# Attention and selective scan on one core: the convolution folded into u's weights, side results used a step later, one product with B per unit

## The chip, the core and the metric

The kernel runs on one core of one Trainium2 chip. The metric is device time in microseconds (us) of one execution of the whole program, all 16 images included. Five engines matter: PE (TensorE: matmuls, with PEld for its weight loads), DVE (VectorE), ACT (ScalarE), POOL (GpSimd) and SP (SyncE), which issues the DMA transfers here. SBUF and PSUM are the core's two on-chip memories; matmuls write PSUM. "f32 128x512" is a tile of 128 partitions with 512 elements each.

## The reference, cut to what matters

The input x is (16, 256, 32, 32). Two layers follow each other, each on a group-normalised x and added to x:

```python
x = x + _L0_conv_ref(_gn(x), ...)   # attention and a feed-forward part
x = x + _L1_conv_ref(_gn(x), ...)   # a selective scan with a gate
```

With 32 x 32 positions there are L = 1024 tokens of 256 channels. Layer 0 adds a position embedding and has layer norm, four heads of attention, layer norm and two feed-forward products with gelu. Layer 1 is, cut to its core:

```python
xs = xs + pos
ctx = sigmoid(conv1d(xs, gate_w, width 3) + gate_b)
xz = xs @ in_proj_w.T
u, z = split(xz, 2)                       # 512 channels each
uc = causal depthwise conv(u, conv_w, width 4) + conv_b
u = silu(uc)
dt, Bm, Cm = split(u @ x_proj_w.T, [16, 80])
delta = softplus(dt @ dt_proj_w.T + dt_proj_b)
A = -exp(A_log)                           # 512 x 64
def step(h, inp):                         # over the 1024 tokens
    dA = exp(d_t[..., None] * A)
    h = dA * h + (d_t * u_t)[..., None] * B_t[:, None, :]
    y = einsum('bdn,bn->bd', h, C_t)
y = (ys + u * D) * silu(z)
return (y @ out_proj_w.T) * ctx
```

## The kernel before, in words

**The main loop.** The scan has 512 channels x 64 states x 1024 steps for every image. It is cut into units: for each of the 16 images (b), 2 halves of the tokens (t), 4 blocks of 128 channels (k), 4 quarters of a block (q) and 8 groups (i): 256 units per image, 4,096 in all. A unit scans four channels over 512 tokens: two instructions of 128 partitions (two channels x 64 states each) x 512. In iteration n the loop body issues, in this order: `load(n+6)`, `inputs(n+4)`, the two scans of unit n, `decay(n+2)`, then steps of the side work, then the steps of the output generators that are running.

- `load` fetches delta*u of the unit's channels, repeated over the 64 states, in one DMA of 512 KB into `dub` (L859, seven buffers), and at block edges B, C and the pieces of delta.
- `inputs` multiplies `dub` by B on POOL, in place, in two instructions of 128x512, one for each scan (L869).
- `decay` makes delta*A: two matmuls that pick rows out of `pieces` (L878) into two of four PSUM buffers, and two Exp on ACT in place (L881).
- `scan` runs the recurrence on DVE: h = a*h + dub (L891), into one of two h buffers.
- `outputs`, once per eight units, forms y = C*h: 128 small matmuls per half (L928) against the spread C (`cd`), a copy on ACT (L936), small matmuls that turn the result (L940), a copy to `yo` (L948) and four stores on SP (L954), a step apart.
- `spread_c` makes `cd` once per t: eight ACT instructions in unit 6 (L907). When t is 0 a memset of the whole `cd` on POOL goes first (L903). The PSUM tile `yb` is cleared on DVE per t (L918).

**The side work.** While image b is scanned, the main loop also prepares image b+1 and finishes image b-1. This is one chain of generators: `first_norm` (group norm), `gate_and_store(b-1)` (output product and gate), `attention_layer`, `scan_inputs`. Each `yield` in them carries a share of work; the loop advances the chain at an even rate, so that a step falls into about every unit, and all of it ends before the image's last units. Image 0 is prepared alone, before the first scan (the prologue); the last image's loop has only `gate_and_store` beside it.

All of PE, ACT, DVE and POOL keep the order in which the program issues (a dependency is added from each instruction to the next of its engine at the end of the program). So an instruction that waits holds up everything behind it on its engine. SP's order is set by the scheduler.

**Lines that the change and the prediction touch.** In `group_norm` the variance goes through Ln and Exp on ACT (L260 to L261) and is used by DVE (L264) one step later; `layer_norm` has means (`ln_m`, matmuls L272), differences (L279), variances (`ln_v`, L272), Ln and Exp (L298) and the products (L303); `gate_and_store` adds u*D and gates by z (L787, L791), makes the output product (`m_ps`, L816) and finishes it (L803, L805). In `scan_inputs`:

- z: per 128 channels and half, two matmuls (L607), Tanh on ACT (L612), and DVE's product (L596), issued at the next half's start. L584 adds the position before.
- u: per 128 channels and half two matmuls (L628), a copy with three zeros ahead of it (L633) and the last tap with its bias on ACT (L634); then three taps of 128x1024 on DVE (L642), Tanh on ACT (L679) and one product on DVE (L682).
- the gate's convolution: eight groups of 12 matmul instructions and a bias (L657, L661), beside the taps.
- dt, B and C: `x_ps` (L694, L698).
- softplus and the pieces of delta, per 128 channels: matmul (L713), ACT (L715, L722, L739), DVE (L726, L727, L743, L748, L752, L756) and stores on SP.

PSUM has eight banks: four for the decays (`aps`), one for `yb`, one `accp` for the attention's accumulation, two (`mm`) for all other side matmuls through `psum`. `wide` has ten buffers of 128 x 1030.

## Time and profile before

| what | value |
|---|---|
| median of four runs | 13,538.78 us (13,537.11 to 13,545.84) |
| the profiled execution, its own time | 13,537.89 us |
| its span (first to last instruction) | 13,536.1 us |
| granted TensorE clock, mean | 0.767 |
| busy PE, PEld | 10,665.2 us (79%), 5,378.5 us (40%) |
| busy DVE | 12,099.6 us (89%) |
| busy ACT | 7,914.7 us (58%) |
| busy POOL | 10,458.8 us (77%) |
| DMA | 2,821.36 MB, 208 GB/s over the span |

How to read what follows: a group line of the profile has the source line, the engine, the operation, output and inputs with their shapes, the number of executions; after the first bar the busy time in us and the mean of one in ns; after the second bar the engine's idle time just before these instructions, and what ended most of it. "<-POOL dub L869" means that the engine idled until POOL's instruction of line 869 had written `dub`. A window line has its bounds in us from the span's start, its length, then busy time and number of instructions for each engine, the granted PE clock (1.00 is full speed), the share of the DMA engines' time, and GB/s. A timeline line has the start in us, the duration of the run of equal instructions, the engine, line and operation, their number, and in brackets the idle time before.

By the scans' places in the trace, the first scan starts at 387.8 us and the last ends at 13,488.1 us. The loop over the first image takes 794.6 us, over each of the images 1 to 14 about 831 us, and over the last 672.9 us.

### The profile page before, as it was taken

To read this page: it belongs to the slowest core of one execution; us is meant where nothing else is said; L and a number is where in the kernel's file an instruction comes from. 1 tells how busy PE (TensorE), PEld (TensorE's weight loads), DVE (VectorE), ACT (ScalarE), POOL (GpSimd) and SP (SyncE) were. 2 spreads that over 40 slices of the span, in tenths; PEclk is the share of its full clock that TensorE was granted. 3 is DMA by queue.
4 is the path that set the end of the run, shared out by engine and by line. 5 is a ranking of instruction groups with operands and counts; after the bars stand their busy time and mean duration, and the time that the engine had idled before them with its cause. 6 is when DMAs were issued, how large, how long until landed. Compare 5 with 4: busy or idle time off the path is not lost. (4 is left out here: it accounts for less than half of the span.)

```text
span 13536.1 us, 437083 instructions
## 1 busy us (share of the span) xinstructions
PE 10665.2 (79%) x186800; PEld 5378.5 (40%) x186800; DVE 12099.6 (89%) x11683; ACT 7914.7 (58%) x13941; POOL 10458.8 (77%) x8214
## 2 busy tenths in 40 slices
PE   7787878878787787877878778787887878878767
PEld 3343344433444334443344434434444343433434
DVE  3899999899998989999898998999998998899998
ACT  3666665656656566555656556566565665656644
POOL 0687877778777787877878778787787878778888
PEclk8786877868787686876868778687786877868767
DMA  1566566565665656656666566655666566566666
GB/s 60 198 212 233 196 214 217 201 230 202 208 219 202 224 200 213 216 203 225 205 228 202 199 222 206 233 197 202 221 209 234 194 213 216 203 231 202 205 218 224
DMA packets 1001958, 2821.36 MB, mean 208 GB/s; under 512 B 175810, under 2 KB 319427, under 8 KB 1000004
## 3 DMA queue, kind: packets, MB, share of 16 engines
q1 hardware_dynamic: 1000004, 2793.39, 60.5%
q8 instruction: 1460, 23.92, 0.7%
q14 instruction: 494, 4.05, 0.1%
HBM read 2514.18 MB, written 261.62 MB: 205 GB/s over the span
## 5 line engine op out<-in xcount | busy, mean ns | idle before, releaser
L869 POOL TENSOR_TENSOR dub<-dub,bt 128x512 f32<-128x512 f32 x8192 | 10403.6, 1304 | 3024.7 <-DMA dub<-dus 2641.2
L881 ACT ACTIVATE a<-a,acol 128x512 f32<-128x512 f32 x8192 | 5063.3, 659 | 3822.1 <-PE a L878 3790.8
L891 DVE TENSOR_TENSOR_SCAN h<-a,last,dub 128x512 f32<-128x512 f32 x4096 | 4927.4, 1261 | 130.9 <-POOL dub L869 72.6
L891 DVE TENSOR_TENSOR_SCAN h<-a,dub 128x512 f32<-128x512 f32 x4096 | 4692.3, 1201 | 283.3 <-POOL dub L869 212.3
L878 PE MATMUL a<-pieces,pick 48*128 48x512 bf16 x8192 | 2966.6, 467 | 2344.4 <-DVE h L891 2258.4
L928 PEld LDWEIGHTS yb<-h,cd 128*32 128x32 f32 x131072 | 2560.3, 135 | 2036.6 <-issue 1671.8
L928 PE MATMUL yb<-h,cd 128*32 128x64 f32 x131072 | 2957.9, 258 | 147.3 <-DVE yb L918 107.4
L878 PEld LDWEIGHTS <-pick 48*128 48x128 bf16 x8192 | 521.0, 96 | 2513.3 <-issue 2307.7
L403 PE MATMUL s_ps<-k,q 32*64 32x512 f32 x4096 | 888.2, 716 | 58.1 <-DVE mx L384 56.8
L940 PEld LDWEIGHTS yb<-turn,y 128*16 128x16 f32 x32768 | 409.4, 119 | 1011.3 <-ACT y L936 481.4
L936 ACT COPY y<-yb 128x256 f32<-128x256 f32 x1024 | 383.3, 374 | 716.2 <-PE yb L928 711.3
L384 DVE TENSOR_REDUCE mx<-s_ps 128x1 f32<-128x512 f32 x1024 | 644.3, 671 | 22.9 <-PE s_ps L403 20.5
L940 PE MATMUL yb<-turn,y 128*16 128x32 f32 x32768 | 539.2, 212 | 108.0 <-ACT y L936 97.5
L471 PE MATMUL st_ps<-sp 33*128 33x512 f32 x2048 | 598.4, 629 | 17.2 <-ACT pt L479 15.4
L459 PE MATMUL av<-pt,vv 128*64 128x512 f32 x2048 | 582.1, 647 | 5.6 <-ACT sums L448 3.3
L479 ACT ACTIVATE pt<-st_ps 128x512 f32<-128x512 f32 x1024 | 556.7, 605 | 48.2 <-PE st_ps L471 46.8
L657 PE MATMUL g_ps<-w,xp 128*128 128x256 f32 x1536 | 442.8, 443 | 0.0
L403 PEld LDWEIGHTS s_ps<-k,q 32*64 32x64 f32 x4096 | 206.9, 148 | 580.3 <-DVE mx L384 541.5
L657 PEld LDWEIGHTS g_ps<-w,xp 128*128 128x128 f32 x1536 | 387.0, 328 | 96.1 <-issue 74.6
L642 DVE SCALAR_TENSOR_TENSOR u<-up,cwh,u 128x1024 f32<-128x1024 f32 x192 | 295.3, 1538 | 32.7 <-ACT u L634 32.5
L816 PE MATMUL m_ps<-w,xs 128*128 128x256 f32 x1024 | 311.5, 453 | 13.2 <-DVE xs L791 13.2
L816 PEld LDWEIGHTS m_ps<-w,xs 128*128 128x128 f32 x1024 | 259.4, 328 | 90.1 <-issue 60.1
(135 smaller groups left out, 7128.9 us busy)
## 6 DMA issues: line engine op xcount, KB each, us to landing
dub<-dus SPq DMA_DIRECT2D x4096, 512.0 KB
dps<-pc SPq DMA_DIRECT2D x384, 128.0 KB
pieces<-dps SPq DMA_DIRECT2D x1024, 48.0 KB
xs<-in_x_dram SPq DMA_DIRECT2D x64, 512.0 KB
xs<-kept SPq DMA_DIRECT2D x64, 512.0 KB
zs<-z SPq DMA_DIRECT2D x64, 512.0 KB
ud<-u SPq DMA_DIRECT2D x64, 512.0 KB
dus<-du SPq DMA_DIRECT2D x64, 512.0 KB
```

Of the source, the lines that this page charges most:

```text
L384: nc.vector.tensor_reduce(mx[:, g, c, hf : hf + 1], s, AX.X, ALU.max)
L403: nc.tensor.matmul(waiting[g][0][ts(e, 64)], q4[r, ts(c, 64)], k4[r, hs(hf)], start=True, stop=True,)
L459: nc.tensor.matmul(av[ts(e, 2 * DH)], vv[j // (NJ // 2)][:, j % (NJ // 2), 2 * pair + e, :], pts[e], start=(j == 0), stop=(j == NJ - 1),)
L471: nc.tensor.matmul(s, ka[r, ts(j, P)], qa[r, hs(hf)], start=True, stop=True)
L657: nc.tensor.matmul(ps[:, ts(q, C)], xp[k][:, ds(first + t, P, 4)], wg_s[:, k, t, :], start=(i == 0), stop=False,)
L816: nc.tensor.matmul(ps[:, ts(q, C)], us[d][:, ds(first, P, 4)], wo_s[:, d, :], start=(d == 0), stop=(d == ND - 1),)
L869: nc.gpsimd.tensor_tensor(v, v, blocks[b, t]["bt"], ALU.mult)
L878: nc.tensor.matmul(a, w, pieces[r], start=True, stop=True)
L881: nc.scalar.activation(a, a, AF.Exp, scale=acol[:, at : at + 1])
L891: nc.vector.tensor_tensor_scan(now["h", q % 2][:, 2 * i + e, :], decays[n][e], loaded[n][:, e, :], first, ALU.mult, ALU.add,)
L928: nc.tensor.matmul(yb[ts(g, 32), ts(s, 64)], cd[:, at // 16, ts(c, 32)], hbuf[:, :, at : at + 4], start=(c == 0), stop=(c == 3),)
L940: nc.tensor.matmul(out4[32 * s : 32 * s + 16, half, e], y2[:, 64 * s + e : 64 * s + 64 : 4], turn[:, e], start=True, stop=True,)
```

## The change: what it does

- **u.** The depthwise convolution is linear, so it is moved into the input product: the prologue multiplies `w_in`'s columns for u by each of the four taps, on POOL, and stores the 4 x 512 KB of products in DRAM (`wcv`). Per image they are fetched one block at a time into a `wide` buffer (an eleventh is added), and `project` runs eight matmuls per block and half, on four shifted views of xs, in two groups of four with a step between them. Tanh and Identity on ACT and one product of 128x512 on DVE (`finish_u`, a step later) complete u. The copies, the taps and the 128x1024 product are gone, and `weights` fetches only z's half of `w_in`.
- **The gate's** matmuls move from the taps' steps to softplus, in pieces of three or four.
- **Side results a step later.** A `yield` is added between Ln/Exp and their use in `group_norm` and `layer_norm`; the two means of `layer_norm` get a bank each; z's product, m_ps's end and parts of softplus move one step on; `psum3` hands out the two `mm` banks and `accp` in turn for these.
- **B.** `inputs` issues one POOL instruction per unit, 128 x 2 x 512, with B repeated by a stride of zero.
- **cd and yb** are allocated and cleared once, in the prologue; the spread of C is divided over units 5 and 6.
- **Stores of y** are issued two steps later.

```diff
+    cd = hst.tile([P, TB // 16, P], F32, name="cd", tag="cd")
+    nc.gpsimd.memset(cd, 0.0)
...
+        t = work("wcs").rearrange("p (k t e) -> p k t e", k=KC, t=CONV)
+        for k in range(KC):
+            nc.gpsimd.tensor_tensor(
+                t[:, k], row[:, ts(d % 2, CONV * P)].rearrange("p (t e) -> p t e", t=CONV),
+                wu[:, k, ts(d, P)].unsqueeze(1).to_broadcast([P, CONV, P]), ALU.mult,
+            )
+        nc.sync.dma_start(wcv[ts(d, P), :], t.rearrange("p k t e -> p (k t e)"))
...
+    three = cycle((mm, mm, accp))
...
         nc.scalar.activation(v, v, AF.Exp, scale=-0.5)
-        yield 1.5
+        yield 1.2
+        yield 1
...
-        m = mean_of([t[:, hs(0)] for t in src], "ln_m")
-        yield 1
-        q0 = centre(0, m)
-        m = mean_of([t[:, hs(1)] for t in src], "ln_m")
+        m0 = mean_of([t[:, hs(0)] for t in src], "ln_m")
+        yield 0.7
+        m1 = mean_of([t[:, hs(1)] for t in src], "ln_m")
+        yield 0.7
+        q0 = centre(0, m0)
         yield 1.2
-        q1 = centre(1, m)
         vs = [mean_of(q0, "ln_v")]
+        q1 = centre(1, m1)
...
-                finish_z()
-                ps = psum("z_ps")
+                finish_z(1)
+                ps = psum3("z_ps")
...
-            ps = psum("u_ps")
-            for k in range(KC):
+            w = wcs[d].rearrange("p (k t e) -> p k t e", k=KC, t=CONV)
+            ps = psum3("u_ps")
+            for i in range(KC * CONV):
+                k, t = divmod(i, CONV)
                 nc.tensor.matmul(
-                    ps, win_s[:, k, ts(d, P)], body[k][:, hs(hf)],
-                    start=(k == 0), stop=(k == KC - 1),
+                    ps, w[:, k, t], xp[k][:, ds(hf * HL + t, HL)],
+                    start=(i == 0), stop=(i == KC * CONV - 1),
                 )
-            last = d * CONV + CONV - 1
-            nc.scalar.copy(ups[d][:, ds(CONV - 1 + hf * HL, HL)], ps)
-            nc.scalar.activation(
-                us[d][:, hs(hf)], ps, AF.Identity,
-                bias=cbh[:, d : d + 1], scale=cwh[:, last : last + 1],
-            )
+                if i == CONV - 1:
+                    yield 1.3
+            t = hwork("u_t")
+            nc.scalar.activation(t, ps, AF.Tanh, bias=cbh[:, d : d + 1])
+            nc.scalar.activation(ps, ps, AF.Identity, bias=cbh[:, d : d + 1])
+            ready.append((d, hf, t, ps))
...
-            items = [more(d, *items[0]), begin(d, 1)]
-            yield 1
+            items[0] = more(d, *items[0])
+            yield 0.8
+            items.append(begin(d, 1))
+            rest(*items[0])
+            yield 1.3
             items[1] = more(d, *items[1])
-            rest(*items[0])
-            yield 1.4
+            yield 0.8
             rest(*items[1])
...
+            gate(d // 2, d % 2, 0, 0)
             yield 1.4
...
-                    if q == 0:
+                    if q == 1:
                         finish()
...
-        for e in range(2):
-            v = loaded[n][:, e, :]
-            nc.gpsimd.tensor_tensor(v, v, blocks[b, t]["bt"], ALU.mult)
+        v, bt = loaded[n], blocks[b, t]["bt"]
+        nc.gpsimd.tensor_tensor(v, v, bt.unsqueeze(1).to_broadcast([P, 2, TB]), ALU.mult)
...
-        yield
+        for _ in range(3):
+            yield
...
-        if (k, q, i) == (0, 0, 6):
-            spread_c(b, t)
+        if (k, q) == (0, 0) and i in (5, 6):
+            spread_c(b, t, ((0, 1), (2, 3))[i - 5])
```

## The prediction

> **What bounds the kernel now.** I read the busy table first: DVE 12,099.6 of 13,536.1 us (89%), PE 79%, POOL 77%, ACT 58%. No engine is full, so I read DVE's waits next, then the stages, then single places. The costliest groups of the page:
>
> ```profile
> L869 POOL TENSOR_TENSOR dub<-dub,bt 128x512 f32<-128x512 f32 x8192 | 10403.6, 1304 | 3024.7 <-DMA dub<-dus 2641.2
> L891 DVE TENSOR_TENSOR_SCAN h<-a,last,dub 128x512 f32<-128x512 f32 x4096 | 4927.4, 1261 | 130.9 <-POOL dub L869 72.6
> L642 DVE SCALAR_TENSOR_TENSOR u<-up,cwh,u 128x1024 f32<-128x1024 f32 x192 | 295.3, 1538 | 32.7 <-ACT u L634 32.5
> ```
>
> A unit (two scans) needs 2 x 1.304 = 2.61 us of POOL and about 2.4 us of DVE; the scans wait little for POOL. DVE loses more in the side work, by shape:
>
> ```profile
> L726 DVE SCALAR_TENSOR_TENSOR d_ps<-sp_s,d_ps 128x512 f32<-128x512 f32 x128 | 88.4, 691 | 147.9 <-ACT d_ps L722 147.6
> L596 DVE SCALAR_TENSOR_TENSOR z<-z_t,z_ps 128x512 f32<-128x512 f32 x128 | 87.0, 680 | 96.3 <-ACT z_t L612 94.7
> L303 DVE TENSOR_TENSOR xn<-xn,ln_v 128x512 f32<-128x512 f32 x128 | 81.3, 677 | 105.1 <-ACT ln_v L298 105.1
> L264 DVE TENSOR_TENSOR gn<-gn,gn_v_ps 128x1024 f32<-128x1024 f32 x32 | 38.6, 1209 | 95.3 <-ACT gn_v_ps L261 95.3
> L803 DVE SCALAR_TENSOR_TENSOR m_ps<-xs,m_ps 128x512 f32<-128x512 f32 x64 | 44.5, 695 | 90.8 <-PE m_ps L816 90.8
> ```
>
> The last numbers are DVE's idle time: a side operation is placed in the same step as what it consumes, and since DVE keeps program order, the next scans queue behind it. Stage by stage, for image 6 (attention values; the u stage; x; softplus):
>
> ```profile
> core 0: us, PE busy (x) PEld busy (x) DVE busy (x) ACT busy (x) POOL busy (x), PEclk, DMA share, GB/s
> 5628.92:5773.05 144.13, 129.85 (x2638) 62.55 (x2638) 127.59 (x115) 119.63 (x229) 135.15 (x110) 0.94 0.66 221
> 5927.45:5998.10 70.65, 60.87 (x953) 39.48 (x953) 69.31 (x61) 40.08 (x67) 64.11 (x44) 0.91 0.57 189
> 5998.10:6022.93 24.83, 24.83 (x383) 13.38 (x382) 18.36 (x17) 11.24 (x21) 18.48 (x16) 0.97 0.56 199
> 6022.93:6147.99 125.06, 88.38 (x1536) 43.34 (x1535) 115.18 (x121) 90.65 (x151) 86.19 (x71) 0.56 0.60 202
> ```
>
> The bound changes: POOL leads the attention values (135.2 of 144.1), DVE the u stage (69.3 of 70.7), PE all of x, and in softplus DVE idles 9.9 of 125.1. Single places, from timelines:
>
> ```profile
> 6007.37 3.18 PE L694 MATMUL x_ps<-u,w 128*16 128x512 f32 x7
> ...
> 12839.00 3.51 POOL L903 MEMSET cd<- 128x4096 f32 x1
> ...
> 12845.61 4.57 DVE L891 TENSOR_TENSOR_SCAN h<-a,dub 128x512 f32<-128x512 f32 x4 [9.85 <-POOL dub L869]
> ...
> 12902.64 14.41 DVE L787 SCALAR_TENSOR_TENSOR xs<-xs,vec 128x1024 f32<-128x1024 f32 x1
> ```
>
> An f32 matmul of 512 columns is two PE instructions, and those of x start .43 us apart at full clock. The cd memset stops POOL, and DVE after it for 9.85 us. The xs operation, whose fastest execution is 1.25 us, took 14.4 us while POOL ran products without a break: its two inputs both lie in SBUF.
>
> **The change part by part, per image.** Fifteen images carry side work; each idle sum above is divided by 16, since the prologue or the last image adds a sixteenth.
>
> *Side results a step later.* The group norm's Ln and Exp get a whole step before DVE's multiply. Before: 95.3/16 = 6.0 (first norm), 42.2/16 = 2.6 (second). The cd memset, once per image, goes too, and its spread is halved over two units. I take -5.5 and -2.3; bounds are 0 and the rows. m_ps finished a step later: 5.7, I take -5. The layer norms (L303 6.6, L279's wait for ln_m 4.0) with q/k products a step apart: I take -6 for the first and -4 for the second with the steps around it; bounds 0 and -12.1 together, with f_ps's 24.6/16 = 1.5. z: 94.7/16 = 5.9, I take -5. Softplus, L726: 147.6/16 = 9.2, I take -7. None goes whole: the consumer is still in order on DVE, and what is late next is the scan's own inputs (POOL's product, the decay's exp).
>
> *Convolution in u's weights.* Out go 12 taps (1.51 us here) and four 1.31 us products, 23.3 us of DVE; in come eight 128x512 products at .68 like L596, 5.4. DVE of the u and x stages falls from 87.7 to about 69.8 us of 95.5. But PE gets 8 x 8 matmuls for 8 x 2: 128 instructions at .43 = 55.0 us against 13.8. The gates leave for softplus: eight of 12 instructions, 3.15 us each where they run together, 25.2. PE: 60.9 + 24.8 - 13.8 - 25.2 + 55.0 = 101.7 us, against 95.5 of wall. So the bound moves to PE and the saved DVE time is worth nothing: +5 (bounds 0, if the PE's records overlap as the modelled ends allow, and +10). Behind a group of four such matmuls (3.4 us) stand the next unit's decay matmuls, and behind those exp and scan; only two units of lead cover it. In softplus the gates' PE time fits (88.4 + 25.2 = 113.6 of 125.1), but at its clock of .56 a gate step can hold a decay for 3 us: +4 (0 to +13). u's weights arrive by four 512 KB fetches on SP ahead of need, while w_in's fetch is halved; the mean DMA share there is .57, so nothing, or +1 if a dub load waits behind one.
>
> *One product with B per unit.* A 128x1024 product with B repeated has no row. Least: 2 x 1.25 (the fastest halves) less a fixed .2 (the trace's smallest memsets take about .1) = 2.3; most: above 2 x 1.304 = 2.61. The repeat itself seems free: L264 repeats an operand and takes 1.21 us where L791's fastest is 1.19. I take 2 x 1.25 less one start of .1 = 2.40, nearest to the fastest halves. In the attention values 52 units x (2.50 - 2.40) = 5.2, and one join with its load instead of two: -6; v_ps a step later -2; the cd spread in two parts -2: -10 (-12 to 0). ACT at 119.6 and DVE at 127.6 of 144.1 are next.
>
> *The longer lock.* Sixteen DVE operations per image that read two SBUF inputs (L787, L791, L584, L330, L515) wait on average about .3 us for the running product (L791: 1556 mean against 1191 least). With a product twice as long the rest doubles: 16 x .3 = +5.5 with the first ones' worse wait (0 to +12). The taps, which paid this too, are gone.
>
> The Trainium skill, "SBUF — State Buffer", section on separate sides, has the rule behind this row: a VectorE instruction with two SBUF inputs and a GpSimd instruction exclude each other for the whole of whichever started first. It speaks against the longer product; taken strictly the mean wait would double, as in the sentence above, and this trace's 14.41 us says it can be worse. The same skill's "GPSIMD Engine Reference", section 3.1, gives 4497 ns for 2048 elements; with the halves' 1.25 us a straight line through both is an estimate of 2.33 us at 1024, by which the attention values would gain about 2 us more per image. No run here shows it.
>
> *Stores of y two units later* put the SP's wait for yo (564.6 us in all) behind two more loads; the scans waited for POOL only 284.9 us altogether, so I count nothing; without that slack it is at most 284.9/16 = 17.8 per image of POOL starving, in either direction.
>
> Sum: -5.5 - 2.3 - 5 - 6 - 4 - 5 - 7 + 5 + 4 - 10 + 5.5 = -30.3 us per image, x15 = -455. The prologue (first scan at 387.8 us) gains eight POOL products (8 x 1.27 = 10.2) with DMA trips around them, say +12, and u's 128 instructions, 55 us against 39 from u's first matmul to its last product: +14; +26 (0 to +60), all uncovered since no scan runs. The last image has no prepare, loses one memset stall (9.85): -10. Together -439. The profiled execution took 13,537.9 (span 13,536.1), .9 below the median of four runs, 13,538.8: **13,100 us**.
>
> **The rivals.**
> (a) *Half of the gain* : the product costs its pair's mean, 2.61 us, so the attention values keep POOL as their bound (-2 instead of -10), and the PE-bound stage and the lock come at their upper ends (+10, +10): -12.8 per image, -192 + 16 = 13,360. For it: PE 24.83 of 24.83 in x. Against: the fastest halves.
> (b) *More* : waits go nearly whole, the u stage costs nothing: -45 per image, -675 + 16: 12,880. For it: the waits' rows sum to 40 us per image. Against: the next input is late soon after.
> (c) *Slower, by POOL alone* : a product of 2.9 us. The place is each stretch with units of about 2.5 us: 52 attention-value units, some 25 others per image, 220 units of the last image. Each .1 us above 2.5 costs 7.7 us per image, x15 + 22 = 138 us; without POOL's gains the rest is -20 x 15 + 16 = -284; so it decides from 2.5 + .21 = 2.71 us, and 2.9 gives 13,805. For it: halves up to 2.41 us, so products are held up as well, and the repeated operand. Against: same elements, one start fewer.
> (d) *The change does not separate the steps* : step sizes are fractions and several may fall in one unit; then the waits stay, the u stage costs +10 and the time is about 13,536 + 15 x 5 + 26, near 13,640. Against: the built order puts consumers a unit later.
>
> **How the numbers follow.** Forecast .56 (own range 12,980 to 13,230), (a) .17, (b) .13, (c) .10, (d) .04. About 0.2% (27 us) is what a measurement can tell from no change. Faster: .56 + .13 + .17 less a little of (a)'s upper tail = .84; slower .13, same .03. Leaving out (c), (d) and the outer tails of (a) and (b), about .2: 12,870 to 13,420.
>
> **What would show it.** In the changed profile: POOL's group at 4,096 executions near 2,400 ns (2,710 or more: (c)); DVE's waits at the softplus, z, norm and m_ps lines cut to a third; the u and x stages PE-bound at some 100 us with DVE near 70; L787's successor longer than 2,522 ns on average; DVE busy about 200 us lower (17.9 of taps x 16, less the longer lock); first scan near 414 us; image period near 800 us against 831. Wrong would be: waits that reappear at the scans for POOL or for the exp, of the size of those removed, or a half-clock u stage: 55 us more per image, against which x's full clock speaks.

## The result: no gain, and the profile after

The changed kernel takes 13,571.7 us (median of 33 runs, 13,529.7 to 13,606.7), the kernel before in the same comparison 13,548.1 us (54 runs). The ratio is 1.0016, 95% interval 1.0011 to 1.0021: 0.16% slower where 13,100 us had been forecast. The profiled execution took 13,556.6 us, its span is 13,554.8.

The single terms look as if the change had worked. From the page of the changed kernel (first line) and its DVE groups by shape:

```profile
L912 POOL TENSOR_TENSOR dub<-dub,bt 128x1024 f32<-128x1024 f32 x4096 | 9670.4, 2377 | 3795.9 <-DMA dub<-dus 3211.1
L639 DVE SCALAR_TENSOR_TENSOR z<-z_t,z_ps 128x512 f32<-128x512 f32 x128 | 85.7, 670 | 26.1 <-ACT z_t L654 26.1
L345 DVE TENSOR_TENSOR xn<-xn,ln_v 128x512 f32<-128x512 f32 x128 | 80.9, 675 | 36.7 <-ACT ln_v L339 36.7
L304 DVE TENSOR_TENSOR gn<-gn,gn_v_ps 128x1024 f32<-128x1024 f32 x32 | 38.6, 1208 | 11.2 <-ACT gn_v_ps L300 11.2
L847 DVE SCALAR_TENSOR_TENSOR m_ps<-xs,m_ps 128x512 f32<-128x512 f32 x64 | 43.5, 680 | 35.8 <-PE m_ps L860 35.8
```

The product with B costs 2.377 us (2.40 forecast, two halves 2.61), and the waits at z, the norms and m_ps fell from 94.7, 105.1, 95.3 and 90.8 us to 26.1, 36.7, 11.2 and 35.8. The same view shows what rose:

```profile
L934 DVE TENSOR_TENSOR_SCAN h<-a,last,dub 128x512 f32<-128x512 f32 x4096 | 4934.2, 1262 | 556.1 <-issue 304.9 <-POOL dub L912 222.5 <-ACT a L924 25.7
L934 DVE TENSOR_TENSOR_SCAN h<-a,dub 128x512 f32<-128x512 f32 x4096 | 4698.4, 1201 | 345.6 <-issue 221.2 <-POOL dub L912 120.3 <-ACT a L924 0.8
L761 DVE SCALAR_TENSOR_TENSOR d_ps<-sp_s,d_ps 128x512 f32<-128x512 f32 x128 | 89.1, 696 | 238.1 <-ACT d_ps L757 238.1
L667 DVE SCALAR_TENSOR_TENSOR u<-u_t,u_ps 128x512 f32<-128x512 f32 x128 | 86.8, 678 | 166.2 <-ACT u_ps L686 166.2
```

The scans come in two rows: those of the second half of the tokens read `last` and wait 556.1 us (130.9 before), those of the first half wait 345.6, where the kernel before has

```profile
L891 DVE TENSOR_TENSOR_SCAN h<-a,dub 128x512 f32<-128x512 f32 x4096 | 4692.3, 1201 | 283.3 <-POOL dub L869 212.3 <-issue 69.4 <-ACT a L881 0.7
```

Softplus's first DVE operation waits 238.1 (147.6 before), and the new product of u 166.2. The windows of image 6, in the order shown of before (attention values, u, x, softplus):

```profile
5658.00:5806.47 148.47, 136.91 (x2640) 65.51 (x2641) 127.86 (x115) 119.87 (x230) 127.68 (x55) 0.90 0.65 219
5953.37:6038.58 85.21, 80.99 (x1002) 37.65 (x991) 56.02 (x51) 36.28 (x66) 53.84 (x23) 0.96 0.59 196
6038.58:6063.56 24.98, 22.84 (x302) 9.12 (x301) 16.88 (x15) 11.56 (x22) 14.14 (x7) 0.93 0.47 160
6063.56:6190.96 127.40, 103.21 (x1640) 62.72 (x1640) 114.96 (x121) 92.34 (x154) 83.83 (x36) 0.75 0.62 204
```

In the attention values POOL went from 135.2 to 127.7 us busy and the window from 144.1 to 148.5 (in the mean of images 2 to 13, in the table below, the stage did not change). In the u window DVE lost 13.3 us of work, and PE is busy for 81.0 of 85.2 us. The lengths of the two u windows cannot be held against each other: that of before starts 7.8 us behind u's first matmul (5919.65) and ends 9.3 us ahead of x's first (6007.37), that of after holds all of u's matmuls. From u's first matmul to x's first, image 6 took 87.7 us before and 83.7 after, with fewer scans beside it.

**Where the time went, per image.** I sum, over images 2 to 13, DVE's work, its idle time ahead of side operations and its idle time ahead of scans (records of neighbouring DVE instructions overlap slightly, so idle sums can be a little negative). DVE's work: 804.3 to 785.0 us, -19.3. Waits for side results: 33.2 to 22.6, -10.6. Waits of the scans: -6.4 to +24.6, **+31.0**. Together +1.1 of an image period of 831.2. The change freed 30 us per image on DVE, and the scans waited them away.

**What the scans wait for.** The trace says "POOL" and "issue". Comparing each scan's start with the end of its own Exp and of its own product tells otherwise: of 912 us of scan waits over .12 us after the change, 885 end within .3 us of the scan's Exp, with the product done at least half a microsecond earlier (before: 409 of 484). A timeline of *before*, in the attention values:

```profile
5657.37 0.39 PE L878 MATMUL a<-pieces,pick 48*128 48x512 bf16 x2
...
5657.40 3.75 POOL L869 TENSOR_TENSOR dub<-dub,bt 128x512 f32<-128x512 f32 x3 [0.68 <-DMA dub<-dus]
...
5657.83 1.24 ACT L881 ACTIVATE a<-a,acol 128x512 f32<-128x512 f32 x2
...
5658.58 2.34 DVE L891 TENSOR_TENSOR_SCAN h<-a,dub 128x512 f32<-128x512 f32 x2 [0.88 <-issue]
```

The first of the two Exp ends at 5658.49, the scan starts at 5658.58. The product it uses had ended 8.6 us earlier (in the mean of this window 8.8, 5.9 at least); what POOL runs here is for scans that are units away. The same in the u stage after:

```profile
5969.92 3.70 PE L678 MATMUL u_ps<-xp,xs 128*128 128x512 f32 x8
...
5973.55 0.39 PE L921 MATMUL a<-pieces,pick 48*128 48x512 bf16 x2
...
5973.87 3.70 PE L678 MATMUL u_ps<-xp,xs 128*128 128x512 f32 x8
...
5974.01 1.24 ACT L924 ACTIVATE a<-a,acol 128x512 f32<-128x512 f32 x2 [1.97 <-PE a L921]
...
5974.76 2.46 DVE L934 TENSOR_TENSOR_SCAN h<-a,last,dub 128x512 f32<-128x512 f32 x2 [0.76 <-issue]
```

Eight u instructions (3.70 us), decay matmuls, Exp, scans: the two scans take 2.46 us and cannot start sooner than this chain of PE, ACT and DVE allows.

### The profile page after: what moved, and what is told of

The parts are those of the page before. It is cut to its first block, busy times and chain, and to the rows that moved or that the text cites. A ratio compares the mean times of both kernels' runs of the same rounds, so it can differ in the third digit from the quotient of the medians.

```text
span 13554.8 us, 432127 instructions
## 1 busy us (share of the span) xinstructions
PE 11147.4 (82%) x188338; PEld 5588.2 (41%) x188338; DVE 11800.1 (87%) x11460; ACT 7821.7 (58%) x13878; POOL 9684.3 (71%) x4111
## 5 line engine op out<-in xcount | busy, mean ns | idle before, releaser
L912 POOL TENSOR_TENSOR dub<-dub,bt 128x1024 f32<-128x1024 f32 x4096 | 9670.4, 2377 | 3795.9 <-DMA dub<-dus 3211.1
L934 DVE TENSOR_TENSOR_SCAN h<-a,last,dub 128x512 f32<-128x512 f32 x4096 | 4934.2, 1262 | 556.1 <-issue 304.9
L934 DVE TENSOR_TENSOR_SCAN h<-a,dub 128x512 f32<-128x512 f32 x4096 | 4698.4, 1201 | 345.6 <-issue 221.2
L921 PE MATMUL a<-pieces,pick 48*128 48x512 bf16 x8192 | 2730.9, 450 | 1907.7 <-DVE h L934 1877.2
L965 PEld LDWEIGHTS yb<-h,cd 128*32 128x32 f32 x131072 | 2490.9, 132 | 1799.1 <-issue 1637.5
L965 PE MATMUL yb<-h,cd 128*32 128x64 f32 x131072 | 2881.7, 254 | 55.5 <-issue 50.6
L678 PE MATMUL u_ps<-xp,xs 128*128 128x512 f32 x2048 | 978.3, 623 | 35.9 <-DMA xs<-wcv 35.9
L678 PEld LDWEIGHTS u_ps<-xp,xs 128*128 128x128 f32 x2048 | 382.3, 196 | 505.7 <-issue 447.7
L699 PE MATMUL g_ps<-w,xp 128*128 128x256 f32 x1536 | 558.5, 513 | 8.4 <-ACT g L707 8.4
L699 PEld LDWEIGHTS g_ps<-w,xp 128*128 128x128 f32 x1536 | 414.8, 327 | 241.0 <-issue 196.5
L860 PE MATMUL m_ps<-w,xs 128*128 128x256 f32 x1024 | 313.8, 455 | 11.4 <-DVE xs L835 11.4
```

The source lines that it names most:

```text
L678: nc.tensor.matmul(ps, w[:, k, t], xp[k][:, ds(hf * HL + t, HL)], start=(i == 0), stop=(i == KC * CONV - 1),)
L699: nc.tensor.matmul(ps[:, ts(q, C)], xp[k][:, ds(first + t, P, 4)], wg_s[:, k, t, :], start=(k == 0 and t == 0), stop=False,)
L912: nc.gpsimd.tensor_tensor(v, v, bt.unsqueeze(1).to_broadcast([P, 2, TB]), ALU.mult)
L921: nc.tensor.matmul(a, w, pieces[r], start=True, stop=True)
L934: nc.vector.tensor_tensor_scan(now["h", q % 2][:, 2 * i + e, :], decays[n][e], loaded[n][:, e, :], first, ALU.mult, ALU.add,)
L965: nc.tensor.matmul(yb[ts(g, 32), ts(s, 64)], cd[:, at // 16, ts(c, 32)], hbuf[:, :, at : at + 4], start=(c == 0), stop=(c == 3),)
```

## The experiments

Two measures are used below. *Beyond the scans*: the wall time between two landmarks of the side work (first matmul of z to first of u, and so on), less the scans' own durations in between, mean of images 2 to 13; it does not depend on which units a stage falls into. *The rate*: the shares of one image's side work, summed (gate and output product with their 26.6 included) and divided by 247 units, as the loop has it; 1.1109 before, 1.1158 after.

| us per image beyond the scans | before | after | change | forecast |
|---|---|---|---|---|
| first norm | 17.7 | 14.4 | -3.3 | -5.5 |
| gate, m_ps | 20.9 | 19.6 | -1.3 | -5 |
| layer norm 1, q and k | 12.5 | 8.2 | -4.3 | -6 |
| max pass | 34.4 | 33.6 | -0.8 | 0 |
| attention values | 15.2 | 15.1 | -0.1 | -10 |
| output, layer norm 2, feed-forward | 17.1 | 17.9 | +0.8 | -4 |
| second norm | 12.5 | 9.9 | -2.6 | -2.3 |
| z | 9.8 | 6.6 | -3.2 | -5 |
| u and x | 29.7 | 39.3 | +9.6 | +5 |
| softplus with the gates | 33.0 | 38.8 | +5.8 | -3 |
| the longer lock | in the rows above | | | +5.5 |
| all, with the plain scans at the end | 200.9 | 201.3 | +0.4 | -30.3 |

### Parts alone, and the convolution undone

**e1_no_conv**: the changed kernel with u, the taps, the gates beside them and the prologue as before.

```diff
-                yield from project(d, hf)
-                finish_u(1)
-                yield 1.5
+                tap(d, t)
+                if d + 1 < ND:
+                    project(d + 1, t)
+                yield 1.6
```

> The changed kernel with the convolution alone put back as it was (u by two matmuls, taps on DVE, gates beside the taps, no product weights in the prologue); everything else of the change stays. Theory A (the gain of the other parts is real and the convolution eats it: from the changed trace the u stage takes 85.7 us per image against 71.1, softplus with the gates 129.5 against 125.1, the prologue 32 us more): 13,555 - 15 x 18 - 32 = about 13,250, u stage back at 71 us. Theory B (the convolution costs the predicted +5 per image and +26; the other parts never gave their 35 us): 13,555 - 75 - 32 = about 13,450.

Measured: 13,699.4 us, ratio to before 1.011 (1.0094 to 1.0125). Both theories miss, and on the slow side: taking the convolution out made the changed kernel *slower*. Softplus rose to 47.3 us beyond the scans, attention values to 18.2, u to 30.0.

**e2_conv_alone**: the kernel before with the convolution, the gates' new place and the prologue's products.

```diff
+            for i in range(KC * CONV):
+                k, t = divmod(i, CONV)
                 nc.tensor.matmul(
-                    ps, win_s[:, k, ts(d, P)], body[k][:, hs(hf)],
+                    ps, w[:, k, t], xp[k][:, ds(hf * HL + t, HL)],
```

> The kernel before with the convolution alone changed (with the gates in softplus and the prologue's products). Theory A: +15 us in the u stage, +3 to +5 in softplus per image, x15, and +30 for the prologue: 13,538 + 300 = about 13,840. Theory B: +5 per image and +28: about 13,640. In either case DVE busy falls by some 250 us, so a longer time means that DVE's saved work was worth nothing.

Measured: 13,708.6 us, 1.0112 (1.0093 to 1.0132), between the two. u and x +3.3 (28.0 and 5.0), softplus with the gates +6.2, layer norm 2 and feed-forward some 7, but attention values -3.8, with not one line of them changed. That was the first sign of the rate: here it is 1.098.

**e3_b_alone**:

```diff
-        for e in range(2):
-            v = loaded[n][:, e, :]
-            nc.gpsimd.tensor_tensor(v, v, blocks[b, t]["bt"], ALU.mult)
+        v, bt = loaded[n], blocks[b, t]["bt"]
+        nc.gpsimd.tensor_tensor(v, v, bt.unsqueeze(1).to_broadcast([P, 2, TB]), ALU.mult)
```

> The kernel before with one product with B per unit, nothing else. Theory A (in images 1 to 14 the product lies 9 us ahead of its scan and holds nobody; scans in the attention values wait for the decay's Exp; only the last image runs at POOL's pace): attention values unchanged at 145 us, image period 831 within 2, last image 673 - 35 = about 638, sum 13,500. Theory B (POOL bounds the attention values, as predicted): that stage falls by 5 or more to 140, and the longer lock adds 5 elsewhere; sum about the same, 13,500, so the stage table decides and not the sum.

Measured: 13,631.3 us, 1.0056 (1.0035 to 1.0076), where both theories had 13,500. The stage table decides as said: attention values 16.5 against 15.2, so POOL was not their bound and theory A holds there. What A had left out is the longer lock on the taps. DVE groups of this kernel, to be held against 1538 (L642, shown of before) and 1470 ns (L682, where the kernel before has 94.1 us):

```profile
L642 DVE SCALAR_TENSOR_TENSOR u<-up,cwh,u 128x1024 f32<-128x1024 f32 x192 | 348.7, 1816 | 31.7 <-ACT u L634 31.5
L682 DVE SCALAR_TENSOR_TENSOR u<-up,u 128x1024 f32<-128x1024 f32 x64 | 121.1, 1893 | 14.2 <-ACT up L679 14.2
```

That is 53.4 + 27.0 us, and with the other operations that read two SBUF inputs 110 us or 6.9 per image: as much as the 6.3 us per image that this kernel lost. The last image gained 15 us (672.9 to 658.1).

**e4_later_alone**: steps later in the norms, z, m_ps and softplus, nothing else.

```diff
-            items = [more(d, *items[0]), begin(d, 1)]
-            yield 1
+            items[0] = more(d, *items[0])
+            yield 0.8
+            items.append(begin(d, 1))
+            rest(*items[0])
+            yield 1.3
...
-                    if q == 0:
+                    if q == 1:
                         finish()
```

> The kernel before with the later use of side results alone (group and layer norms, z, m_ps, softplus's split; memsets, product with B, convolution and stores as before). Theory A: norms, z and m_ps give 15 to 18 us per image, part of their waits coming back as waits of the scans for Exp; softplus 0 to +4: 13,538 - 15 x 15 = about 13,310. Theory B (the removed waits come back nearly whole as other waits): 13,450 or more. The prediction's own terms would give -26 per image: 13,150.

Measured: 13,764.3 us, 1.0153 (1.0135 to 1.017): slower than the kernel before, so more came back than B's "nearly whole". z fell from 9.8 to 5.0 and both norms' waits as foreseen, but softplus rose by **14.5** (33.0 to 47.5) and the attention values by 3.9. The order of issue shows why: `more` has ACT make an operand, `rest` has DVE use it, and the new share between them is 0.8. This kernel's loop spends 1.129 shares per unit, so the next step falls into the same unit for seven of the eight results of an image (in e1 as well); before, one of eight fell together, six lay one unit apart and one lay two. So in e1 and e4 the split does the reverse of what it is for.

In the changed kernel, at 1.1158 and another phase, only one of eight falls together and seven lie one unit apart: no further than before. Its waits have a second cause, here in unit 217 of image 6:

```profile
6093.34 2.34 PE L699 MATMUL g_ps<-w,xp 128*128 128x256 f32 x5
...
6095.61 1.22 PE L705 MATMUL g_ps<-gate_b,one_row 1*128 1x256 f32 x2
...
6096.76 0.61 PE L921 MATMUL a<-pieces,pick 48*128 48x512 bf16 x2
...
6097.44 1.24 ACT L924 ACTIVATE a<-a,acol 128x512 f32<-128x512 f32 x2
6098.59 0.63 ACT L756 ACTIVATE sp_s<-sp_e 128x512 f32<-128x512 f32 x1
6099.11 0.66 ACT L757 ACTIVATE d_ps<-d_ps,vec 128x512 f32<-128x512 f32 x1
...
6099.80 0.70 DVE L761 SCALAR_TENSOR_TENSOR d_ps<-sp_s,d_ps 128x512 f32<-128x512 f32 x1 [2.75 <-ACT d_ps L757]
```

The gate's matmuls hold the decay until 6096.76, the Exp follow, and only behind these, in ACT's order, comes the operand of softplus. It was issued one unit before its use, and is late all the same. With the gates and no split (e2) softplus is at 39.2, with both (the changed kernel) at 38.8. By this comparison the gates make the loss and the split does not mend it; what the split costs by itself is seen below (g2, h1).

### Mending single parts

**f1_split_apart**: the changed kernel with

```diff
-            yield 0.8
+            yield 1.2
```

at both places of softplus.

> The changed kernel with softplus's two shares of 0.8 raised to 1.2. The loop spends about 1.12 shares per unit, so a step of 0.8 lets the next one fall into the same unit: in the changed trace all eight uses of a softplus result per image stand in the unit of the ACT instruction that makes it (six of eight before). Theory A (these pairs are why softplus got slower): DVE's wait for d_ps falls from 238 to under 60 us, softplus loses 8 us per image, of which 3 come back because the even rate rises by 1.2%: 13,572 - 75 = about 13,500. Theory B (the gates' matmuls in softplus are the cause, in front of the decays): the wait for d_ps goes down but the scans' waits rise by as much, 13,570.

Measured: 13,610.5 us, 1.0036 (1.0024 to 1.0048). (The expectation read the units by the time at which ACT ran; in the order of issue it is one of eight, as told above, and none with 1.2.) The place answers, the sum does not:

```profile
L761 DVE SCALAR_TENSOR_TENSOR d_ps<-sp_s,d_ps 128x512 f32<-128x512 f32 x128 | 89.0, 696 | 155.1 <-ACT d_ps L757 155.1
```

238.1 fell to 155.1 us (A had under 60), softplus to 31.9 beyond the scans. (f4, which has no gates in softplus, also has 31.9: by this comparison the gates' matmuls cost nothing there when there is this much room.) But the shares added raise the rate to 1.129, and the attention values go from 15.1 to 18.8, u from 32.1 to 34.0: the gain is given back.

**f2_early_fetch**:

```diff
         for d in range(ND):
+            if d == 1:
+                fetch(wcs, wcv, 0)
             z = work("z")
...
-        fetch(wcs, wcv, 0)
         finish_z()
```

> The changed kernel with the first block of u's product weights fetched six steps earlier, during z. In the changed trace that fetch is issued 7.3 us ahead of its first matmul, PE waits for it, starts the u stage at half clock, and the unit around it is 5 us longer than before. Theory A (that start costs 5 us per image): the stall goes, 13,572 - 75 = about 13,495, u stage 78 instead of 83 us. Theory B (PE bounds the whole stage, so a late start of u only moves work): the stage keeps its 83 us within 2, time within 30 us of the changed kernel.

What it mends, in the changed kernel's timeline:

```profile
5957.72 6.57 PE L678 MATMUL u_ps<-xp,xs 128*128 128x512 f32 x8 [1.47 <-DMA xs<-wcv]
...
5966.45 2.46 DVE L934 TENSOR_TENSOR_SCAN h<-a,last,dub 128x512 f32<-128x512 f32 x2 [5.93 <-POOL dub L912]
```

The fetch had been issued at 5950.4. PE idles for it, and the first group then takes 6.57 us where later ones take 3.70, so the scans stand for 5.93. Measured: 13,534.7 us, 0.9986 (0.9972 to 1.0). The u stage falls by 1.0 us of wall and 3.3 beyond the scans (32.1 to 28.8). Between the theories: the wait for the fetch goes, and PE's own work keeps the stage at 82.2 us. The first group stays slow in most images; g2 comes back to it.

**f3_kept_parts**: the kernel before with later norms, z and m_ps, one memset and later stores, without convolution, product in one and split.

```diff
+    cd = hst.tile([P, TB // 16, P], F32, name="cd", tag="cd")
+    nc.gpsimd.memset(cd, 0.0)
...
-                finish_z()
-                ps = psum("z_ps")
+                finish_z(1)
+                ps = psum3("z_ps")
...
-        yield
+        for _ in range(3):
+            yield
```

> The kernel before with only the parts that gave something by the stage tables: later use in the group and layer norms, z and m_ps, one memset of cd and yb, stores of y later; no convolution, no product with B in one, no split of softplus. Theory A (these gain 10 us per image, the last image 25): 13,545 - 150 - 25 = about 13,370. Theory B (what they gain is given back wherever the rate, 1.1206 shares per unit against 1.1109, puts steps closer): 13,500 or more.

Measured: 13,471.5 us, 0.9938 (0.9921 to 0.9954), between the two. Per image -6.0, but the last image got 12 us longer and the first norm 5.1. Its timeline at the start of image 6:

```profile
5337.57 17.22 POOL L886 TENSOR_TENSOR dub<-dub,bt 128x512 f32<-128x512 f32 x14
...
5346.90 8.98 DVE L347 TENSOR_TENSOR xs<-xs,gn 128x1024 f32<-128x1024 f32 x1
```

At an image's edge units follow at 2.35 us and POOL needs 2.5, so it falls behind and then runs without a break. I read it so that the stall at the memset used to give it time (no run tests that by itself, and e4, which keeps the memset, has 2.87 us in the mean for this operation, against 1.45 before and 4.47 here). With the stall gone, the operation that reads two SBUF inputs meets a row of 14 products and waits until POOL runs dry. It takes 1.2 us when free.

**f4_kept_and_split_apart**: the same with softplus split at shares of 1.2.

```diff
+            items[0] = more(d, *items[0])
+            yield 1.2
+            items.append(begin(d, 1))
+            rest(*items[0])
+            yield 1.3
```

> The same with softplus split as in the change, but with shares of 1.2 in place of 0.8. Theory A: softplus at or below its 119 us before (138 with the split's own shares), so within 60 us of the run without the split, either way; the even rate rises to 1.142. Theory B (the split itself is the loss, not its shares): softplus stays near 138 us and the time is about 200 us above the run without it.

Measured: 13,564.2 us, 1.0002 (0.9992 to 1.0011), 93 us above f3, where A had allowed 60. Softplus is 31.9 beyond the scans, against 30.7 without the split: no gain. Rate 1.142: attention values 18.0, u 27.2.

### What the product with B and the size of a step do

**g1_kept_and_b** (f3 with the product in one):

```diff
-            nc.gpsimd.tensor_tensor(v, v, blocks[b, t]["bt"], ALU.mult)
+        nc.gpsimd.tensor_tensor(v, v, bt.unsqueeze(1).to_broadcast([P, 2, TB]), ALU.mult)
```

> The kept parts (later use in the norms, z and m_ps, one memset, later stores) and the product with B in one; no convolution, no split of softplus. Theory A (the product pays only where units follow each other at DVE's pace: at an image's edge and in the last image; with the kept parts alone POOL had fallen behind there, and one xs operation of 8.98 us at unit 11 waited for 14 products in a row): unit 11 falls from 11.1 to under 5 us, the last image from 685 to about 635, the taps get 4 us per image longer as in the run with B alone: 13,472 - 15 x 3 - 50 = about 13,375. Theory B (POOL's pace does not matter in these places): 13,472 + 15 x 4 = 13,530.

Measured: 13,480.5 us, 0.9943 (0.9926 to 0.9959). The places came nearly as A said (unit 11 from 11.1 to 3.8 us, last image 685 to 647 for A's 635), but the taps under the longer lock took u from 24.0 to 31.7, not 4 more: nothing is left.

**g4_no_b** (the changed kernel with the product in halves):

```diff
-        nc.gpsimd.tensor_tensor(v, v, bt.unsqueeze(1).to_broadcast([P, 2, TB]), ALU.mult)
+            nc.gpsimd.tensor_tensor(v, v, blocks[b, t]["bt"], ALU.mult)
```

> The changed kernel with the product with B back in two halves, all else as changed. Theory A (as above): attention values as before within 2 us per image (POOL held nobody there), image edge +5 to +8 at the xs operations, last image 634 + 45: 13,572 + 15 x 6 + 45 = about 13,705. Theory B (POOL bounds the attention values): that stage rises by 5 to 10 us besides, 13,800 or more.

Measured: 13,614.2 us, 1.0046 (1.0031 to 1.0061). Attention values 14.9 against 15.1: POOL held nobody there. The last image takes 682 in place of 634, and the xs operation of the first norm has 1.8 times its time, 1413 ns in the changed kernel:

```profile
L372 DVE TENSOR_TENSOR xs<-xs,gn 128x1024 f32<-128x1024 f32 x32 | 81.6, 2554 | 0.0
```

So A by its places, with less per image than it said. The product in one is worth some 40 us in the whole program, at the edges, and only where no taps suffer from it.

**g2_early_fetch_no_split** (f2 with softplus in its old steps):

```diff
-            items[0] = more(d, *items[0])
-            yield 0.8
-            items.append(begin(d, 1))
-            rest(*items[0])
-            yield 1.3
+            items = [more(d, *items[0]), begin(d, 1)]
+            yield 1
             items[1] = more(d, *items[1])
-            yield 0.8
+            rest(*items[0])
+            yield 1.4
             rest(*items[1])
```

> The changed kernel with the early fetch of u's weights and with softplus in its old steps (the gates stay there). Theory A (with the gates there the split as it was cost nothing net, 39.4 us of softplus beyond the scans with it and 39.2 in the convolution alone without it; the rate falls from 1.116 to 1.108): softplus 37 to 40, attention values 2 us lower, 13,535 - 15 x 3 = about 13,490. Theory B (the split is the loss in the changed kernel): softplus falls by 6 us, 13,535 - 15 x 6 = 13,445 or less.

Measured: **13,403.2 us, 0.9898 (0.9883 to 0.9912)**: theory B, and 1.2% below the changed kernel. Yet softplus itself gave 3.2 of the 11.4 us per image (39.4 to 36.2). The attention values gave 4.8 (15.5 to 10.7) and u 2.3, with their code untouched and the rate down to 1.108. More than half of u's part is the granted PE clock at its start. In f2 PE idles 1.71 us ahead of u's first eight instructions, and these take 5.0 us in the mean of the loops over images 1 to 14 (3.70 in four of them). Here PE idles 1.08 us, and they take 3.70 in every image. For image 6, f2 first:

```profile
5971.62:5977.02 5.40, 5.40 (x13) 2.08 (x16) 4.35 (x4) 1.24 (x2) 2.50 (x2) 0.68 1.00 291
5906.70:5910.40 3.70, 3.70 (x15) 1.50 (x18) 3.70 (x4) 1.24 (x2) 2.35 (x1) 1.00 0.98 272
```

**g3_small_groups** (f2 with u in four steps of two matmuls):

```diff
-                if i == CONV - 1:
-                    yield 1.3
+                if i % 2 == 1 and i < KC * CONV - 1:
+                    yield 1.2
...
-                yield 1.5
+                yield 1.2
```

> The changed kernel with the early fetch, and u's eight matmuls per half in four steps of two (shares 1.2) instead of two steps of four. The u stage then spreads over some 33 units in place of 20. Theory A (the u stage is bound by PE's 83 us, so what counts is how many scans run beside them): time beyond the scans of that stage falls from 28.8 to 15 or less, while the even rate rises by 7% and costs the attention values 5 to 10 us per image: sum between -10 and +3 us per image, 13,535 - 50 = about 13,485, within 120. Theory B (a scan waits whenever matmuls stand between two decays, whatever their number): beyond-scan time stays at 28 or grows, 13,650 or more.

Measured: 13,490.2 us, 0.996 (0.9945 to 0.9975), as A said. u takes 33 units and 11.1 us beyond the scans in place of 28.8; the rate of 1.181 takes 5.1 back in the attention values and 4.1 in the max pass.

### The rate by itself

**h1_lower_rate** (f2, split kept):

```diff
-            rate, due = total / (UNITS - AHEAD - 3), 0.0
+            rate, due = total / (UNITS - AHEAD - 1), 0.0
```

> The changed kernel with the early fetch, its split of softplus kept, and the even rate divided by 249 in place of 247 units: 1.107 shares per unit, as without the split. Theory A (the split costs mostly by its extra shares, which push everything else closer): attention values and u fall as without the split (10.7 and 26.5 us beyond the scans, from 15.5 and 28.8), 13,535 - 15 x 7 = about 13,430. Theory B (the split costs by itself, by which steps meet in a unit): 13,520 or more, softplus still at 38 to 40 us beyond the scans.

Measured: 13,440.8 us, 0.9917 (0.9902 to 0.9932): theory A. Attention values 10.2, u 26.2, softplus still 38.8. One number in the pacing is worth 0.7% of f2's time; the split in itself costs the 2.6 us per image that remain to g2's softplus.

**h2_no_split_groups_of_two** (g2, u in steps of two, rate over 249 units):

```diff
-            rate, due = total / (UNITS - AHEAD - 3), 0.0
+            rate, due = total / (UNITS - AHEAD - 1), 0.0
...
+                if i % 2 == 1 and i < KC * CONV - 1:
+                    yield 1.2
```

> Early fetch, softplus in its old steps, u in steps of two matmuls, the rate over 249 units (1.163). Theory A (PE-bound stages gain by lying beside more scans): u 11 us beyond the scans against 26.5, softplus 36 against 36.2, attention values and max 8 us dearer by the rate: 13,403 - 15 x 5 = about 13,330. Theory B (the even rate takes it all back): 13,400 to 13,480.

Measured: 13,491.6 us, 0.9954 (0.9937 to 0.997). u 11.8, as in g3, and everything else dearer (max 38.3, attention values 15.6, layer norm 2 16.7): theory B, a little above its upper end.

**h3_no_split_lower_rate** (g2, rate over 249 units, 1.099):

```diff
-            rate, due = total / (UNITS - AHEAD - 3), 0.0
+            rate, due = total / (UNITS - AHEAD - 1), 0.0
```

> Early fetch, softplus in its old steps, u in its steps of four, the rate over 249 units (1.099 against 1.108). Theory A (a slower pace alone is worth something, about 3 us per image per percent in the PE-bound stages): 13,403 - 15 x 2.5 = about 13,365. Theory B (only which steps meet in a unit counts): any change between -60 and +60, with stages changing sign among themselves.

Measured: 13,407.3 us, 0.9891 (0.9876 to 0.9907), the same as g2. A slower pace alone is worth nothing more here; theory B.

The attention values, whose own code only the product with B touches, against the rate:

| rate | kernels | us beyond the scans |
|---|---|---|
| 1.098 to 1.108 | e2, h3, h1, g2 | 11.4, 10.4, 10.2, 10.7 |
| 1.111 to 1.121 | before, e3, after, f2, g4, f3, g1 | 15.2, 16.5, 15.1, 15.5, 14.9, 16.1, 16.3 |
| 1.129 to 1.181 | e1, e4, f1, f4, h2, g3 | 18.2, 19.1, 18.8, 18.0, 15.6, 20.6 |

There is a step between 1.108 and 1.111, and a drift above it that is not strict (h2). Which two steps meet at that step I have not traced. That the rate itself is the cause is not shown: a new rate also moves every step to other units, and the stage's granted PE clock goes with the rows in part (means of .914 to .928 in the first, .878 to .907 in the last; but the kernel before has .918 at 15.2 us).

## Why the prediction was wrong, point by point

**The step that failed: each freed wait and each saved DVE operation was booked as time.** The sum was -30.3 us per image, and the table has +0.4. DVE's work did fall by 19.3 us and its waits for side results by 10.6, and the scans waited 31.0 longer, nearly all of it for their Exp. The prediction had named this as its sign of being wrong ("waits that reappear at the scans for POOL or for the exp, of the size of those removed") and had given it no price. It also took it that a side operation stands "in the same step as what it consumes"; by the order of issue the group norm's and nearly all of z's uses lay one unit behind already, and lie two behind after.

**"In the attention values 52 units x (2.50 - 2.40) = 5.2 ... -10": wrong, -0.1.** The price was right (2.377 us), the bound was not. I took POOL's 135.2 busy us of 144.1, and the releaser "POOL dub" of the scans, for a bound. The products were nearly 9 us ahead of their scans. The scan waits for two semaphores and the profile named the wrong one. e3 and g4 show it from both sides. (The estimate of 2.33 us from the Trainium skill's "GPSIMD Engine Reference", section 3.1, would have made 52 x .07 = 3.6 us more, not 2; nothing hangs on it, for the bound was wrong.)

**"Softplus, L726 ... I take -7", and "+4" for the gates: wrong, +5.8 together.** The gates in their new place cost 6.2 (e2), because a gate step stands ahead of a decay, and ACT makes softplus's operands behind that decay's Exp. I had counted the delay of a decay, not that the result meant to come early waits behind it. And the -7 had no ground: the split gave no distance, for six of the eight uses of an image had lain one unit behind already, and seven do so after. By g2 and h1 it costs 2.6 to 3.2 us. My rival (d), steps that fall into one unit, came true in e1 and e4 (+14.3 and +14.5), not in the changed kernel.

**"+5 (bounds 0 ... and +10)" for u and x: the mechanism right, the size off, +9.6.** PE did become the bound: 81.0 us busy of 85.2. Its sum over u and x, 103.8, is near the 101.7 worked out. The 95.5 us of wall that this was held against left out the start of u, as told above. What was missing is the late fetch, 3.3 us (f2). I had counted its transfer, not its arrival: SP issued it 7 us ahead of its first matmul. And a PE-bound stage should be priced by the scans that fit beside it, not by its wall (g3: 94.9 us of wall, but 11.1 beyond the scans).

**"m_ps ... I take -5" and "-4" for the second layer norm: the waits went and came back.** At m_ps DVE's wait fell from 5.7 to 2.2 us per image, while the scans of the same units now wait 3.2, none before; and the gate's first operation (`xs<-xs,vec`) waits 70.5 us for its fetch of u in place of 33.1, which no term had counted. It rises wherever the later steps are (70.2 in e4) and not in e2 or e3 (14.2 and 28.7); why is open. From the attention's output to the feed-forward part the side waits fell by some 7.5 and the scans' waits rose by 5.9. "What is late next" was said to be product or Exp; by the ends of both operands it was Exp.

**First norm, second norm, layer norm 1, z: right in kind**, -13.4 of the -18.8 forecast.

**"16 x .3 = +5.5" for the longer lock: the sign right, the size off.** (16 x .3 is 4.8; the rest is "the first ones' worse wait".) In images 1 to 14 the 16 operations took 24.9 us per image in place of 23.7, +1.2. In the last image they fell from 66.9 to 39.3 us, which is part of its gain. With the taps the lock cost 6.9 (e3): the two parts of the change need each other.

**What I had not counted at all: the rate.** The added yields bring 4.4 shares and the convolution takes 3.2 away, so that the sum without gate and output product goes from 247.8 to 249.0. That rise itself cost the attention values nothing (15.2 before, 15.1 after). But the early fetch with the rate 0.8% lower, h1, takes 0.7% less than f2: a gain lay below both rates.

**Ends:** the first scan came 31.9 us later (26 forecast). The first image's loop took 14.5 us longer, the images 1 to 14 together 14.0, and the last image 39.3 less (10 forecast). It is the place where POOL's pace counts most: g4, with halves, has 682 us there.

Sum: +31.9 + 14.5 + 14.0 - 39.3 = +21.1 us at the last scan, against -439.

## What to carry to other kernels

When the profile says that an engine waits for a producer, compare the waiting instruction's start with the end of *each* of its operands before pricing a faster producer. In an order kept by hand, a freed wait is worth only what the next input of the same chain allows; price that input (here decay matmul, Exp, scan) before counting the gain. And a paced schedule is a resource of its own: a share below the rate pairs steps that were to be apart, and a share added anywhere packs all other stages closer.

## What the runs showed of the hardware that was not expected

- A DVE operation with two SBUF inputs can wait for a whole row of POOL products: 8.98 us in a row of 14 (f3, image 6), 14.41 in the last image of the kernel before. It is not the rule. Where another product followed at once, f3 has 20 such long waits, and 184 times the operation ended between the two products, the second of which then takes over 1.8 us in place of 1.25. What parts the two cases no run shows. The Trainium skill, "SBUF — State Buffer", section on separate sides, has the exclusive lock per instruction; these traces add that the side that waits may be passed over more than once.
- The repeated operand costs POOL nothing: 128x1024 takes 2.329 us at least (median 2.354), less than two halves of 1.250 (median 1.268). The straight line through the halves and the figure of the Trainium skill's "GPSIMD Engine Reference", section 3.1, had given an estimate of 2.33.
- A short idle of PE is enough to halve the granted clock for a while. After 3.2 us of idle in three pieces (.91, .80 and 1.47 for the fetch) the eight u instructions of image 6 took 6.57 us at a mean clock of .56, and 3.70 at 1.00 later. In f2 1.71 us of idle out of the 3.41 us ahead were followed by half clock for 3.41 us in image 6, and ten of fourteen loops have a first group of 5.3 us or more; in g2, with 1.08 us of idle, none has.
